# Batch 0 of the one-head layer: its weighted sums by seven block products, and batch 1's norm moved ahead into layer 1's end and batch 0's scores

## The chip, the cores and the metric

The kernel runs on one core of a Trainium2 chip. The metric is the device time of one execution in microseconds (us). The time before is the median of three runs; a profile was taken of one further execution, and every detailed number below comes from that one.

## The reference

Four layers run one after the other on `x`, four batches of 512 channels by 1024 places, all in f32:

```python
x = _L0(x)   # attention with 8 heads of 64, and x added
x = _L1(x)   # linear attention: softplus features, a gate of max + mean, and x added
x = _L2(x)   # layer norm over channels, attention with ONE head of 512, and x added
x = _L3(x)   # group norm, attention with 4 heads of 128, and x added

# _L2, per batch, xf = places x channels
mu = mean(xf, -1);  var = var(xf, -1)
xn = (xf - mu) * rsqrt(var + eps) * norm_w
q, k, v = split(xn @ w_qkv.T + b_qkv)
attn = softmax(q @ k.T * 512 ** -0.5)
out = x + ((attn @ v) @ w_proj.T + b_proj)
```

The change is in layer 2 (`_L2`) and in the end of layer 1 for the last batch.

## The kernel before, in words

**Paths.** `plain_path` computes everything without subtracting row maxima from the scores, and records whether all sums stayed in range; `general_path` follows only where they didn't. With these inputs only `plain_path` runs.

**Block products.** A product of two matrices, each cut into 2 x 2 blocks, is made with seven block products instead of eight, at the price of sums of blocks beforehand and of results afterwards. `seven_products` does this for projections and scores, under the names `p1` to `p7`; within one product the names p5, p6, p7 use sums of blocks on both sides, p3 and p4 on one side. A "join" is the addition of a finished block product to the result (lines L746, L783, L789). Accumulators are PSUM tiles `acc`, four of them; a second pool holds two double tiles, tag `sc`, which the scores, the norm's sums (`lnsums`), and layer 1's steps (`kxt`, `kv`, `upd`) share.

**Order of the work.** TensorE's instructions are issued in exactly the order in which the Python code makes them (`tc.manual_schedule`). The order on the other engines is worked out by the framework's scheduler, which also places the semaphores and frees buffers. Small pieces of another batch's work are put between products through a list, `pieces`: each call of `slot()` inside `seven_products` takes one piece. How many slots there are among the first products (p1 and p2) is set by the parameter `slots`; after each pair of the later ones (p3 to p7) there is always one.

**Around the change.** Layer 1 for batch 3 (`linear_attention`, a list `lin` of pieces) runs as such pieces inside layer 2's start: batch 0's projection of queries and of values. Its last five pieces are `transpose_kx`, `keys_times_values`, an idle one, and two `update`s, which add layer 1's result to `x3`. After them `x3` is written to DRAM (`away`) and batch 1's `x` is read back (`back`)[...].

Layer 2 then goes batch by batch, in `for b in range(B)`: queries by `seven_products` (L716), values by `project_v` (L841), then `one_head`: scores by `seven_products` (L848), exponentials (L1246), and the weighted sums. For batches 1 to 3 the weighted sums are made by a second set of seven products, written out in `one_head` (matmuls at L1325, block sums at L1319, joins at L1335, ScalarE copies at L1339), each of two output columns with four matmuls of 128x512: 7 x 2 x 4 = 56. For batch 0 they are made by a plain loop of eight output blocks with eight matmuls each (L1286): 64. Both are followed or interleaved by two row-sum matmuls (L1265), reciprocals (L687) and the final additions to `x` (L1272, L1274).

**The norm of the next batch.** `layer_norm` for one half of 512 places gives four pieces: `add` (three VectorE additions over the channels, L1588 and L1590), `center` (a TensorE sum, L1596; four VectorE centrings, L1598; ScalarE squares, L1603, summed by VectorE, L1607), `spread` (a TensorE sum, L1612; ScalarE's square root, L1614; VectorE's reciprocal, L1615) and `scale` (four VectorE scalings, L1620). Its results go into tiles `after`, which for batch 1 take the buffers of layer 1's weights. For batch 0 these pieces of batch 1 are put between the eight output blocks of the plain loop, through the list `parts`, since batch 1's `x` is on the chip only then; the last of them makes batch 1's input sums (`sum_inputs`, L695 to L698). For batches 1 and 2 they are put among the projection of values and the scores.

**DMA.** All transfers are issued by SyncE's queue, in its order. Layer 1's transposition sends blocks (`squares`) to DRAM (L1458) and loads them back transposed (L1464).

Of the kernel before, what the change touches and what calls it, by code (L numbers as in the profile page):

```python
# [475 lines left out]
def plain_path(ctx: ExitStack, tc: tile.TileContext, d: dict, out: bass.AP, count):  # L476
# [23 lines left out]
    def acc_tile():  # L500
        return ps_acc.tile([P, TB], F32, tag="acc", name="acc")

    def two_tile(name):
        return ps_sc.tile([P, 2, TB], F32, tag="sc", name=name)
# [4 lines left out]
    def pt_tile(name):  # L509
        return work.tile([P, 2, TB], F32, tag="pt", bufs=4, name=name)  # L510
# [15 lines left out]
    def chunks_tile(tag, name, bufs=1):  # L526
        return work.tile([P, NC, TB], F32, tag=tag, bufs=bufs, name=name)
# [7 lines left out]
    def load_wo(src):  # L535
        t = wpool.tile([P, NC, C], F32, tag="wo", name="wo")
        nc.sync.dma_start(t, src.rearrange("(c p) o -> p c o", p=P))
        return t
# [33 lines left out]
    def away(b):  # L572
        homes[b] = dram.tile([P, NC, S], F32, tag=f"home{b}", bufs=1, name=f"home{b}")
        nc.sync.dma_start(homes[b], xs.pop(b))

    def back(b):
        nc.sync.dma_start(x_tile(b), homes.pop(b))
# [97 lines left out]
    def both(*fs):  # L675
        return lambda: [f() for f in fs]
# [8 lines left out]
    def invert(rd, ps):  # L685

        nc.vector.reciprocal(rd, ps)  # L687
        n, m = next(unit), rd.shape[0]
        for i, t in enumerate((ps, rd)):
            closing[:] = [nc.vector.tensor_reduce(tops[:m, i, n : n + 1], t, AX.X, ALU.max).ins]  # L690
# [532 lines left out]
        while parts:  # L1223
            parts.pop(0)()

    def one_head(b, q, ws, acc, xn, sums, v, scale, bias, room, between, parts):

# [13 lines left out]
        def exp(tb, o):  # L1244
# [12 lines left out]
            lambda: sums,  # L1257
            lambda o: ws,
            keys_first,
            done=exp,  # L1260
        )
        def row_sums():
            rows = two_tile("rowsum")
            for t in range(NTB):
                nc.tensor.matmul(  # L1265
                    rows[:, t, :], lhsT=ones, rhs=acc[:, t, :], start=True, stop=True
                )
            return rows

        def add_block(m, tb, t, source, quotient):  # L1270

            nc.vector.tensor_tensor(t, source, quotient, ALU.mult)  # L1272
            xv = x[:, m, bass.ts(tb, TB)]
            nc.vector.scalar_tensor_tensor(xv, t, bias[:, m : m + 1], xv, ALU.add, ALU.add)  # L1274

        flush()
        between()

        if parts:
            rds = chunks_tile("q0", "rd")  # L1280
            for k, (qb, m) in enumerate(itertools.product(range(NTB), range(NC))):
                if parts:
                    parts.pop(0)()
                out = acc_tile()
                for i, j in enumerate(order):
                    nc.tensor.matmul(  # L1286
                        out, lhsT=v[j // 2][:, j % 2, bass.ts(m, P)], rhs=pts[j][:, qb, :],
                        start=(i == 0), stop=(i == NT - 1),
                    )
                if k == 0:  # L1290
                    rows = row_sums()
                if m == 0:
                    invert(rds[:, qb, :], rows[:, qb, :])
                add_block(m, qb, rds[:, NTB + k % 2, :], out, rds[:, qb, :])
            return

# [279 lines left out]
        ]  # L1578


    def layer_norm(b, tb, tiles):

        x = lambda c: xs[b][:, c, bass.ts(tb, TB)]
        t = {}

        def add():
            s = t["s"] = row_tile("s")
            nc.vector.tensor_tensor(s, x(0), x(1), ALU.add)  # L1588
            for c in range(2, NC):
                nc.vector.tensor_tensor(s, s, x(c), ALU.add)  # L1590

        def center():
            xn = tiles[tb]
            t["ps"] = two_tile("lnsums")
            mean = t["ps"][:, 0, :]
            nc.tensor.matmul(mean, lhsT=ones, rhs=t["s"], start=True, stop=True)  # L1596
            for c in range(NC):
                nc.vector.scalar_tensor_tensor(  # L1598
                    xn[:, c, :], mean, -1.0 / C, x(c), ALU.mult, ALU.add
                )  # L1600
            for c in range(NC):
                sq = row_tile("sq")
                nc.scalar.activation(sq, xn[:, c, :], AF.Square)  # L1603
                if c == 0:
                    t["sq"] = sq
                else:
                    nc.vector.tensor_tensor(t["sq"], t["sq"], sq, ALU.add)  # L1607

        def spread():
            xn = tiles[tb]  # L1610
            var = t["ps"][:, 1, :]
            nc.tensor.matmul(var, lhsT=ones, rhs=t["sq"], start=True, stop=True)  # L1612
            rstd = t["rstd"] = row_tile("rstd")
            nc.scalar.activation(rstd, var, AF.Sqrt, bias=eps, scale=1.0 / C)  # L1614
            nc.vector.reciprocal(rstd, rstd)  # L1615

        def scale():
            xn, rstd = tiles[tb], t["rstd"]
            for c in range(NC):
                nc.vector.scalar_tensor_tensor(  # L1620
                    xn[:, c, :], xn[:, c, :], col("nw2", c), rstd, ALU.mult, ALU.mult
                )

        return [add, center, spread, scale]


# [62 lines left out]
    with tc.manual_schedule(engines={mybir.EngineType.PE}):  # L1689
# [52 lines left out]
        for o in gps:  # L1742
# [10 lines left out]
        loadedv = load_bias(d["bv2"], d["wo2n"], vt[2:], brows[:, 1, :])  # L1753
        flush()
        wo2 = load_wo(d["wo2"])
        lin = linear_attention(B - 1, lambda i: pt_tile("l1"))

        norms[1][0]()
        pieces.extend([
            both(*norms[0][2:]), norms[1][1], *lin[:2], both(*norms[1][2:]), idle, *lin[2:]  # L1760
        ])
        gq = chunks_tile("ot", "gq")
        for o in range(NC):
# [21 lines left out]
        for b in range(B):  # L1785
            q = q_tiles()
            vt = v_tiles()
            after = normed_tiles(b + 1)

            def sums():  # L1790
                if b == 0:
                    made.extend(sum_inputs(spare, normed(xn)))
                return made

            half = NC // 2
            seven_products(
                half,
                lambda i, j, o: gq[:, 2 * j : 2 * j + 2, bass.ts(i * half + o, P)],
                normed(xn),
                lambda i, o: uq[:, i * half + o : i * half + o + 1],  # L1800
                lambda i, tb, o: q[tb][:, i * half + o, :],
                sums,
                slots=2,
            )

            pair = lambda t, i: t[:, 2 * i : 2 * i + 2, :]
            halves = work.tile([P, 2, 2, TB], F32, tag="os", name="qs")
            third = work.tile([P, 2, TB], F32, tag="oi", name="qs")
            places = [halves[:, 0], halves[:, 1], third, pair(q[1], 0)]
            sum_weights(places, lambda i, j: pair(q[i], j))  # L1810
            if b == 0:
                pieces.append(lambda: (away(B - 1), back(1)))
            parts = []
            if b + 1 < B:
                (add0, *n0), (add1, *n1) = [layer_norm(b + 1, tb, after) for tb in range(NTB)]
            if b == 0:

                parts = [
                    both(add0, n0[0]), idle, both(*n0[1:], add1), idle, n1[0], idle,
                    both(*n1[1:]), lambda: sum_inputs(spare, normed(after)),  # L1820
                ]
            elif b + 1 < B:
                pieces.extend([
                    add0, n0[0], idle, n0[1], n0[2], add1, n1[0], idle, n1[1], n1[2],
                ])
            else:
                first = chunks_tile("ot", "gn")
                loaded3 = load_bias(
                    d["bv3"], d["wo3n"], [after[1][:, 2 * i : 2 * i + 2, :] for i in range(2)]
                )  # L1830
                loads3 = []
                pieces.extend([
                    *group_norm(0, 0, first),
                    lambda: loads3.append(weighted_bias("bo3", loaded3)),
                ])
            project_v(vt, hv, normed(xn), made, wpool.tile([P, NC, C], F32, tag="wo", name="ws"))
            one_head(
                b, q, places, work.tile([P, 2, TB], F32, tag="ou", name="acc"), xn, made, vt,
                float(C) ** -0.5, bo2,
                after if b == B - 1 else [w2[:, NC : 2 * NC, :], w2[:, 2 * NC :, :]],  # L1840
                lambda: b + 1 < B or loads3.insert(0, load_wqkv(d["wqkv3"])), parts,
            )
            if 0 < b < B - 1:
                sum_inputs(spare, normed(after))
            away(b)
            back((b + 2) % B)
            if b + 1 < B:
                xn = after
# [103 lines left out]
```

## Time and profile before

| | us |
|---|---|
| median of 3 runs (2434.74 to 2436.24) | 2435.08 |
| the profiled execution | 2434.68 |
| its span in the profile | 2433.0 |
| TensorE busy in the span | 2416.0 |
| VectorE busy | 1497.2 |
| ScalarE busy | 697.6 |
| GpSimd busy | 250.8 |

The span runs from the first to the last instruction in the profile; the rest of the execution's time, 1.68 us, lies around it. Times in the views are in us from the span's start. A line such as `L1286` is a line of the kernel before. Names left of the arrow are what an instruction writes, right of it what it reads; `xN` is how many there are, and a bracket gives the idle time of the engine just before and what ended it. PE is TensorE, DVE VectorE, ACT ScalarE, POOL GpSimd, SPq SyncE's queue. An f32 matmul shows as two records.

### The profile page before, as it was taken

What the parts mean: (1) busy time and instruction counts of PE and PEld (TensorE: products, weight loads), DVE (VectorE), ACT (ScalarE), POOL (GpSimd) and SP (SyncE); (2) the same over time, 40 slices, a digit from 0 to 9 for tenths busy, and PEclk for the clock granted to TensorE, in tenths of its full rate; (3) what the DMA queues carried; (4) which work ended last, traced back from release to release, by engine and by line L of the source; (5) the groups of instructions that cost most, each with busy time, mean ns of one, the idle gap of its engine ahead of it and who ended that gap; (6) DMA issues with size and microseconds to landing.
All of it is one profiled execution on the core that took longest, in us unless ns stands there. A gap on an engine that the chain in (4) does not pass through costs nothing.

```text
span 2433.0 us, 24544 instructions
## 1 busy us (share of the span) xinstructions
PE 2416.0 (99%) x10002; PEld 1203.5 (49%) x10002; DVE 1497.2 (62%) x1786; ACT 697.6 (29%) x860; POOL 250.8 (10%) x240
## 2 busy tenths in 40 slices
PE   9999999999999999999999999999999999999999
PEld 4444544453455344544646446455556446555653
DVE  3678577757875789556595775754453554445344
ACT  1454154406431643121211302013321330322132
POOL 4001100110020002102103021021020001002000
PEclk9999999999999999999999999999999999999999
DMA  5001120211022121111001020110110011001001
GB/s 186 9 11 42 46 79 17 55 61 44 19 77 87 58 58 53 44 52 69 1 0 69 5 87 0 52 70 18 35 70 0 18 35 52 1 35 35 1 22 45
DMA packets 41900, 104.35 MB, mean 43 GB/s; under 512 B 3419, under 2 KB 19291, under 8 KB 38838
## 3 DMA queue, kind: packets, MB, share of 16 engines
q1 hardware_dynamic: 41782, 102.73, 12.5%
q8 instruction: 80, 1.31, 0.2%
q14 instruction: 38, 0.31, 0.0%
HBM read 68.98 MB, written 33.74 MB: 42 GB/s over the span
## 4 chain that ended last, share of the span: by engine, by line
PE 98%; DVE 1%; ACT 1%; issue 0%; DMA 0%; SPq 0%; DVEq 0%
PE acc L716 19%; PE acc L841 12%; PE acc L976 9%; PE acc L991 9%; PE sc L945 9%; PE sc L940 9%; PE acc L848 8%; PE acc L1093 7%; PE acc L1325 6%; PE acc L1286 2%; PE acc L1027 1%; PE acc L650 1%; PE upd L1553 1%; PE acc L1493 1%; PE kv L650 1%; PE feat L650 1%
## 5 line engine op out<-in xcount | busy, mean ns | idle before, releaser
L950 ACT ACTIVATE pt<-sc 128x1024 f32<-128x1024 f32 x384 | 379.2, 1022 | 541.2 <-PE sc L945 304.0
L959 DVE TENSOR_TENSOR sum<-sum,pt 128x1024 f32<-128x1024 f32 x256 | 314.4, 1228 | 159.3 <-ACT pt L950 147.2
L976 PE MATMUL acc<-pt,v 64*64 64x512 f32 x2048 | 248.4, 591 | 0.0
L940 PE MATMUL sc<-q,k 64*64 64x512 f32 x2048 | 245.5, 591 | 1.1 <-ACT pt L950 1.1
L991 PE MATMUL acc<-pt,v 128*128 128x512 f32 x512 | 240.8, 594 | 0.0
L945 PE MATMUL sc<-q,k 128*128 128x512 f32 x512 | 239.8, 593 | 0.0
L716 PE MATMUL acc<-t,ws 128*128 128x512 f32 x384 | 173.9, 593 | 0.0
L704 POOL TENSOR_TENSOR ws<-wqkv 128x256 f32<-128x256 f32 (+1 forms) x40 | 39.2, 981 | 1296.7 <-PE acc L1027 516.1
L956 DVE TENSOR_TENSOR sum<-pt 128x1024 f32<-128x1024 f32 x64 | 78.0, 1219 | 137.4 <-ACT pt L950 137.4
L991 PEld LDWEIGHTS acc<-pt,v 128*128 128x128 f32 x512 | 96.6, 190 | 125.3 <-issue 121.6
L945 PEld LDWEIGHTS sc<-q,k 128*128 128x128 f32 x512 | 96.8, 190 | 116.2 <-issue 93.1
L976 PEld LDWEIGHTS acc<-pt,v 64*64 64x64 f32 x2048 | 77.5, 133 | 143.9 <-issue 141.1
L940 PEld LDWEIGHTS sc<-q,k 64*64 64x64 f32 x2048 | 76.9, 133 | 141.8 <-issue 132.9
L716 PEld LDWEIGHTS acc<-t,ws 128*128 128x128 f32 x384 | 72.7, 190 | 88.0 <-issue 87.3
L755 ACT COPY v<-acc 128x512 f32<-128x512 f32 x24 | 14.0, 585 | 305.2 <-PE acc L841 305.2
L687 DVE RECIPROCAL rd<-acc 128x512 f32<-128x512 f32 (+1 forms) x24 | 80.5, 3353 | 29.1 <-PE acc L1027 29.1
L841 PE MATMUL acc<-ws,t 128*128 128x256 f32 x384 | 86.8, 379 | 0.0
L848 PE MATMUL acc<-qs,w 128*128 128x512 f32 x192 | 86.3, 592 | 0.0
L848 PE MATMUL acc<-q,ln 128*128 128x512 f32 x192 | 85.8, 593 | 0.0
L1093 PE MATMUL acc<-ot,wo 128*128 128x256 f32 x336 | 80.6, 383 | 2.7 <-ACT ou L1112 2.7
L746 DVE TENSOR_TENSOR v<-acc,v 128x512 f32<-128x512 f32 x72 | 49.6, 690 | 53.7 <-PE acc L841 53.6
L755 ACT COPY q<-acc 128x512 f32<-128x512 f32 x40 | 23.4, 585 | 195.8 <-PE acc L716 195.8
(323 smaller groups left out, 3420.1 us busy)
## 6 DMA issues: line engine op xcount, KB each, us to landing
home<-x SPq DMA_DIRECT2D x8, 2048.0 KB
x<-home SPq DMA_DIRECT2D x8, 2048.0 KB
squares<-squares SPq DMA_DIRECT2D x32, 256.0 KB
out<-x SPq DMA_DIRECT2D x32, 256.0 KB
rds<-quotients SPq DMA_DIRECT2D x30, 256.0 KB
rds<-quotients SPq DMA_DIRECT2D x7, 1024.0 KB
x<-in_x SPq DMA_DIRECT2D x3, 2048.0 KB
v<-squares SPq DMA_DIRECT2D x12, 512.0 KB
```

Of the source, the lines that this page charges most:

```text
L687: nc.vector.reciprocal(rd, ps)
L716: nc.tensor.matmul(ps, lhsT=w[:, m, :], rhs=x[:, m, :], start=start, stop=stop, skip_group_check=True)
L841: nc.tensor.matmul(ps[:, bass.ts(r, C // 2)], lhsT=x[:, m, bass.ts(2 * o + r, P)], rhs=w[:, m, :], start=(start and r == 0), stop=stop, sk ...
L848: nc.tensor.matmul(ps, lhsT=x[:, m, bass.ts(o, P)], rhs=w[:, m, :], start=start, stop=stop, skip_group_check=True,)
L940: nc.tensor.matmul(ps[half(h), s, :], lhsT=key(g, i)[half(s), half(h)], rhs=q[qb][half(s), g, :], start=True, stop=True,)
L945: nc.tensor.matmul(ps[:, s, :], lhsT=key(g, 2 * i + s), rhs=q[qb][:, g, :], start=True, stop=True)
L950: exps.append(nc.scalar.activation(pt, ps, AF.Exp, scale=scale).ins)
L959: adds.append(nc.vector.tensor_tensor(acc, acc, pt, ALU.add).ins)
L976: nc.tensor.matmul(outs[qb, g][r][half(s), :], lhsT=v[i // 2][half(r), i % 2, g * P + s * hd : g * P + (s + 1) * hd], rhs=pt[half(r), s, : ...
L991: nc.tensor.matmul(outs[qb, g][0], lhsT=v[j // 2][:, j % 2, bass.ts(g, P)], rhs=pt[:, s, :], start=(j == 0), stop=(j == NT - 1),)
L1093: nc.tensor.matmul(ps[i][:, bass.ts(o, n)], lhsT=w[:, m, bass.ts(o, P)], rhs=t[:, m, :], start=(start and m + o == 0), stop=(stop and m == ...
L1325: nc.tensor.matmul(ps[i, o], lhsT=w[m][:, bass.ts(o, P)], rhs=t[m], start=(start and m == 0), stop=(stop and m == 3), skip_group_check=True,)
```

## The change

1. The plain loop over eight output blocks in `one_head` is gone, and with it the parameter `parts`. All four batches take the seven products.
2. Batch 1's norm reads copies of batch 1's `x` instead of the `x` tile. `copy_next` reads one half from DRAM into a buffer, 1 MB each: the first into the buffer of layer 0's shared quotients (tag `rds`), the second into that of layer 1's transposed blocks (tag `many`).
3. The norm's pieces stand among layer 1's last five pieces, in batch 0's projection of values, and among the first products of batch 0's scores. The write of `x3` and the read of batch 1's `x` come after the second half's centring.
4. The scores get four more slots (`slots=NC`), in every batch. Batches 1 and 2 keep their list of norm pieces, so its last ones come at those slots.
5. The norm's two sums take a PSUM tile each instead of sharing one.
6. Batch 1's input sums are made after `one_head`, as for the later batches.

```diff
-    def one_head(b, q, ws, acc, xn, sums, v, scale, bias, room, between, parts):
+    def one_head(b, q, ws, acc, xn, sums, v, scale, bias, room, between):
...
             keys_first,
+            slots=NC,
             done=exp,
         )
...
-        if parts:
-            rds = chunks_tile("q0", "rd")
-            for k, (qb, m) in enumerate(itertools.product(range(NTB), range(NC))):
-                if parts:
-                    parts.pop(0)()
-                out = acc_tile()
-                for i, j in enumerate(order):
-                    nc.tensor.matmul(
-                        out, lhsT=v[j // 2][:, j % 2, bass.ts(m, P)], rhs=pts[j][:, qb, :],
-                        start=(i == 0), stop=(i == NT - 1),
-                    )
-                if k == 0:
-                    rows = row_sums()
-                if m == 0:
-                    invert(rds[:, qb, :], rows[:, qb, :])
-                add_block(m, qb, rds[:, NTB + k % 2, :], out, rds[:, qb, :])
-            return
...
-    def layer_norm(b, tb, tiles):
-        x = lambda c: xs[b][:, c, bass.ts(tb, TB)]
+    def layer_norm(b, tb, tiles, copies=None):
+        x = lambda c: copies[tb][:, c, :] if copies else xs[b][:, c, bass.ts(tb, TB)]
...
-            t["ps"] = two_tile("lnsums")
-            mean = t["ps"][:, 0, :]
+            mean = two_tile("lnsums")[:, 0, :]
...
-            var = t["ps"][:, 1, :]
+            var = two_tile("lnsums")[:, 0, :]
...
+        copies = []
+
+        def copy_next(t):
+            nc.sync.dma_start(t, homes[1][:, :, bass.ts(len(copies), TB)])
+            copies.append(t)
+
+        copy_next(work.tile([P, NC, TB], F32, tag="rds", name="x1"))
         lin = linear_attention(B - 1, lambda i: pt_tile("l1"))
...
-            both(*norms[0][2:]), norms[1][1], *lin[:2], both(*norms[1][2:]), idle, *lin[2:]
+            both(*norms[0][2:]), norms[1][1], *lin[:2], both(*norms[1][2:]), idle, *lin[2:-5]
...
+            if b == 0:
+                (add0, *n0), (add1, *n1) = [
+                    layer_norm(1, tb, after, copies) for tb in range(NTB)
+                ]
+                transpose_kx, keys_times_values, _, *updates = lin[-5:]
+                pieces.extend([
+                    both(transpose_kx, add0),
+                    both(keys_times_values, lambda: copy_next(many_tile("x1"))), n0[0], *updates,
+                    n0[1], both(n0[2], add1), both(n1[0], lambda: (away(B - 1), back(1))), idle,
+                    *n1[1:],
+                ])
...
-            if b == 0:
-                pieces.append(lambda: (away(B - 1), back(1)))
-            parts = []
-            if b + 1 < B:
+            if 0 < b < B - 1:
                 (add0, *n0), (add1, *n1) = [layer_norm(b + 1, tb, after) for tb in range(NTB)]
-            if b == 0:
-                parts = [
-                    both(add0, n0[0]), idle, both(*n0[1:], add1), idle, n1[0], idle,
-                    both(*n1[1:]), lambda: sum_inputs(spare, normed(after)),
-                ]
-            elif b + 1 < B:
                 pieces.extend([
                     add0, n0[0], idle, n0[1], n0[2], add1, n1[0], idle, n1[1], n1[2],
                 ])
-            else:
+            elif b > 0:
...
-            if 0 < b < B - 1:
+            if b < B - 1:
                 sum_inputs(spare, normed(after))
```

More of the change, by code (lines that the diff above doesn't have):

```diff
@@ L1840, in plain_path @@
                 after if b == B - 1 else [w2[:, NC : 2 * NC, :], w2[:, 2 * NC :, :]],
-                lambda: b + 1 < B or loads3.insert(0, load_wqkv(d["wqkv3"])), parts,
+                lambda: b + 1 < B or loads3.insert(0, load_wqkv(d["wqkv3"])),
             )
-            if 0 < b < B - 1:
+            if b < B - 1:
                 sum_inputs(spare, normed(after))
```

## The prediction

> **What bounds the kernel now.** I read the page's busy times and chain first, then the order in time of TensorE and VectorE around layer 2's first batch, then SyncE's queue. From the page:
>
> ```profile
> PE 2416.0 (99%) x10002; PEld 1203.5 (49%) x10002; DVE 1497.2 (62%) x1786; ACT 697.6 (29%) x860; POOL 250.8 (10%) x240
> ...
> PE 98%; DVE 1%; ACT 1%; issue 0%; DMA 0%; SPq 0%; DVEq 0%
> ```
>
> TensorE is the bound almost everywhere: work taken from it counts in full, work given to others counts only where TensorE comes to wait. Busy times by stage: columns are length, then busy us (count) of TensorE, weight loads, VectorE, ScalarE, GpSimd, then clock and DMA.
>
> ```profile
> 1007.00:1048.00 41.00, 41.00 (x139) 23.82 (x138) 16.51 (x23) 5.27 (x9) 0.00 (x0) 1.00 0.26 103
> 1048.00:1078.00 30.00, 30.00 (x72) 13.26 (x71) 18.59 (x26) 8.68 (x8) 0.00 (x0) 1.00 0.00 1
> 1078.00:1138.00 60.00, 60.00 (x142) 26.52 (x141) 48.12 (x55) 8.72 (x12) 2.77 (x3) 1.00 0.00 0
> 1238.00:1288.00 50.00, 50.00 (x117) 21.97 (x117) 41.68 (x57) 2.92 (x4) 4.95 (x5) 1.00 0.00 0
> ```
>
> Rows one and two are the end of layer 1 and batch 0's scores, row three its weighted sums by eight products, row four batch 1's by seven. TensorE is full in all four: seven products already run here without a hole. TensorE in order of time (start, duration, line, records):
>
> ```profile
> 1077.48 1.02 PE L1596 MATMUL lnsums<-s,ones 128*128 128x512 f32 x2
> 1078.34 5.31 PE L1286 MATMUL acc<-pt,v 128*128 128x512 f32 x12
> ...
> 1137.56 7.03 PE L716 MATMUL acc<-ln,gq 128*128 128x512 f32 x16
> ...
> 1188.36 1.12 PE L1596 MATMUL lnsums<-s,ones 128*128 128x512 f32 x2 [0.71 <-DVE s L1590]
> ...
> 1238.25 2.74 PE L1325 MATMUL acc<-pt,v 128*128 128x512 f32 x6
> ...
> 1253.70 3.60 PE L1325 MATMUL acc<-w 128*128 128x512 f32 x8
> ...
> 1288.17 7.03 PE L716 MATMUL acc<-ln,gq 128*128 128x512 f32 x16
> ```
>
> An f32 matmul is two records. Starts, not durations, give its price: batch 1's 56 products and two row sums fill 1238.25 to 1288.17, 49.92 / 58 = 0.86 us each. Batch 0's 64 products, two row sums and three norm sums (69) fill 1078.34 to 1137.56: 59.22 / 69 = 0.858. The bracket at 1188.36 is the one hole in layer 2's batches.
>
> VectorE, in order of time:
>
> ```profile
> 1178.05 3.35 DVE L1615 RECIPROCAL rstd<-rstd 128x512 f32<-128x512 f32 x1 [0.29 <-ACT rstd L1614]
> ...
> 1186.90 1.41 DVE L1590 TENSOR_TENSOR s<-s,x 128x512 f32<-128x512 f32 x2
> ...
> 1235.13 0.68 DVE L746 TENSOR_TENSOR pts<-acc,pts 128x512 f32<-128x512 f32 x1
> ...
> 1249.10 1.42 DVE L1319 TENSOR_TENSOR v<-v,w 128x256 f32<-128x256 f32 x4
> ```
>
> In batch 1 the sums that the norm's mean needs (L1590) stand behind a reciprocal: hence the hole. The seven products' own sums end at 1249.10 + 1.42 = 1250.5, 3.2 us before the first product that needs them (1253.70). SyncE's queue:
>
> ```profile
> 957.62 2.87 SPq L1458 DMA_DIRECT2D squares<-squares  x4
> 960.58 23.07 SPq L1464 DMA_DIRECT2D l<-squares  x4
> ```
>
> [...] (a record shows 592 ns, two start within 858), so I price by starts. [...] four loads at L1464 take SyncE 23.07 us, so a new copy's wait would hold up what follows.
>
> **The change, part by part.**
> (1) 64 products become 56. Row and norm sums keep their number; the issue order has exactly 8 matmuls of 128x512 fewer. 8 x 0.858 = -6.87 us, all on the path.
> (2) The seven products need 16 sums of 128x256 (0.42 us), 16 of 128x512 and 10 joins (0.685): 6.7 + 17.8 = 24.5 us of VectorE, and two ScalarE copies (0.58). Cover: the norm leaves this stretch. A half of it is 3 adds, 4 centrings, 3 square sums (10 x 0.685), a reciprocal (3.35) and 4 scalings (0.68 to 0.9): 13 to 14 us, two halves 27. So VectorE's 18.59 + 48.12 changes by about -2.5.
> (3) Those 27 us move to about 1011 to 1059. There the first row has VectorE busy 16.51 of 41 and GpSimd idle. Cover exists, if each piece is in time.
> (4) Two copies of 1 MB from DRAM, on SyncE's queue. The first goes out once the last shared quotient is read (L1060, 897.5 to 898.7), ahead of loads that left at 902.6; free. The second stands ahead of the four L1464 loads and waits for the block writes issued at 957.62 to 960.5. DMA activity there dies by about 966, first load included. 2 MB take 6.3 us (layer 1's write issued 1031.07, its read 1037.39), so 1 MB is estimated at 3 to 4 us: the first load lands near 971; its products start at 991.55. The second load waits for softplus (near 980) anyway. Price 0, from both sides: no wait is there to be removed, and 20 us of lateness are free.
> (5) Batch 3's write back and batch 1's read move behind the norm. With copies nobody needs that x before batch 1's additions (from 1264). Free.
> (6) Four more slots in the scores. In batches 1 and 2 the second variance comes 8 matmuls after its mean (6.87 us) instead of 24. In batch 2 VectorE's squares were summed at 1344.4, mean finished at 1338.95: 5.5 needed, 1.4 spare. Free.
> (7) In the changed VectorE order batch 1's mean sums stand ahead of the reciprocal, as they already do in batch 2, where TensorE has no hole. The 0.71 us go: -0.71.
> (8) Batch 1's input sums (L695 to L698) no longer come inside batch 0's last products but among its final additions; batches 1 and 2 do this already without a hole. Free.
>
> **The new waits in batch 0,** from the issue orders with the durations above. TensorE, each start the one before plus 0.858 (f32, 512 columns) or 0.43 (256) per matmul: first mean at 1018.3, first updates 1022.6, first variance 1033.3, second mean 1041.0, second variance 1048.8, weighted sums from 1080.5. VectorE fits the first adds into its 2.9 us idle before the key-value step at 1015. The first centrings free a PSUM pair at 1022.4; the second update needs it at 1023.5. First squares at 1024.8: 8 us early. Second adds at 1034.4: 6.6 early. Second squares at 1047.4: 1.4 early. Behind the second reciprocal (1050.5 to 1053.9) stand the joins of p6 and p5; p3 of column 0 needs p5's by 1056.5: 1053.8, p6's join 0.6, p5's 0.6, ready at 1055.0. At the end p3 of the last column, at 1078.8, needs the join of p5, which ends on TensorE at 1077.1. VectorE, free at 1076.8, has two new sums (0.6 each) in front of it, so the join runs 1078.0 to 1078.6: 0.2 spare, against 0.7 in batch 1 (join from 1235.13, p3 from 1236.53). I take 0.1 us of waiting for all of them; the bounds are 0, as nothing waits here now so there is no gain to be had, and about 5 (each of five places a whole late addition or two). The seven products' sums end near 1088; needed at 1096.
>
> Sum: -6.87 - 0.71 + 0.1 = -7.5. Span 2433.0 to 2425.5; that execution's 2434.68 (1.68 around its span) to 2427.2; the median 2435.08, 0.4 above it, to 2427.6.
>
> **Rivals.** (A) Small waits in batch 0's scores. For: VectorE's order is tight (0.2, 1.1, 1.4). Against: each is short and batch 1 has the same pattern. 2 to 5 us lost: 2429.6 to 2432.6, say 2431. (B) VectorE becomes the bound of the weighted sums: the scores' joins slip and the sums with them. For: 42 of 50 us busy in batch 1. Against: 8 us spare. If p6 waits 7 us, the saving is eaten: about 2435. (C) Slower: the second copy blocks SyncE. If its buffer comes free late, the four block loads leave late and layer 1's key products wait at 991.55. It decides where the second load leaves after about 985 + 12.5 us (saving plus 0.2%), 34 later than the block writes land; at 45 later TensorE waits some 23 us: 2450. Against: the buffer's readers are just those block writes. (D) The products stay eight: excluded, the instruction count shows 8 fewer.
>
> **Chances.** Forecast 0.72 (own range 2426 to 2429.5), A 0.15, B 0.05, C 0.05, 0.03 for a larger gain. What a measurement can tell from no change is 0.2%, 4.9 us: below 2430.2 is faster, above 2440 slower. Faster: 0.72 + 0.03 + a third of A = 0.80; slower: C and a tail, 0.06; same 0.14. The range 2425.5 to 2432 leaves out B, C and A's upper end.
>
> **What would show it.** TensorE full from 1007 to the end of batch 0's weighted sums, which take about 49.8 us instead of 59.2; the hole at batch 1's second mean gone; the L1464 line's loads still ending near 983; norm sums of batch 1 between 1018 and 1050. Wrong if brackets naming VectorE appear at lnsums or acc products there, if p3 of the last column waits, or if key products wait for DMA.

## The result and the profile after

| | before | after |
|---|---|---|
| median, us (9 runs of each, side by side) | 2435.66 (2434.69 to 2436.85) | 2428.38 (2427.94 to 2429.06) |
| the profiled execution, us | 2434.68 | 2428.28 |
| its span, us | 2433.0 | 2426.6 |
| TensorE busy, us (records) | 2416.0 (10002) | 2409.3 (9986) |
| VectorE busy, us (instructions) | 1497.2 (1786) | 1520.1 (1828) |

The ratio is 0.997, with a 95% interval of 0.9962 to 0.9979: 7.3 us faster. The prediction was 2427.6 us, 7.5 us faster.

First the page of the kernel after: its busy times, and the shares of the chain that ended last. In every view below, line numbers are those of the kernel that the view is of.

```profile
PE 2409.3 (99%) x9986; PEld 1200.5 (49%) x9986; DVE 1520.1 (63%) x1828; ACT 700.3 (29%) x863; POOL 251.6 (10%) x240
...
PE 98%; DVE 1%; ACT 0%; DMA 0%; issue 0%; SPq 0%; DVEq 0%
```

Sixteen records fewer are eight matmuls fewer. VectorE has 22.9 us more to do and the chain hardly notices: it is TensorE's as before.

Busy times by stage of the kernel after, in the columns of the prediction's table: end of layer 1, batch 0's scores, batch 0's weighted sums, and batch 1's weighted sums.

```profile
1007.00:1048.00 41.00, 41.00 (x140) 24.15 (x140) 33.10 (x45) 11.90 (x19) 0.00 (x0) 1.00 0.26 103
1048.00:1080.00 32.00, 32.00 (x76) 14.11 (x75) 29.30 (x43) 8.31 (x8) 0.00 (x0) 1.00 0.00 1
1080.00:1131.00 51.00, 51.00 (x120) 22.48 (x119) 41.77 (x56) 3.29 (x4) 4.56 (x4) 1.00 0.00 0
1229.00:1281.00 52.00, 52.00 (x122) 22.91 (x121) 42.38 (x56) 3.29 (x4) 4.90 (x5) 1.00 0.00 0
```

TensorE is full in all four. In the first row VectorE goes from 16.51 to 33.10 us: that is the norm. The third row now looks like the fourth.

TensorE in order of time, the kernel after:

```profile
962.24 3.60 PE L716 MATMUL acc<-ln,gq 128*128 128x512 f32 x8
...
1019.03 1.02 PE L1581 MATMUL lnsums<-s,ones 128*128 128x512 f32 x2
...
1049.91 1.02 PE L1597 MATMUL lnsums<-sq,ones 128*128 128x512 f32 x2
...
1079.95 1.88 PE L848 MATMUL acc<-q,ln 128*128 128x512 f32 x4
1081.66 2.74 PE L1308 MATMUL acc<-pt,v 128*128 128x512 f32 x6
...
1131.59 1.88 PE L716 MATMUL acc<-ln,gq 128*128 128x512 f32 x4
...
1181.51 1.02 PE L1581 MATMUL lnsums<-s,ones 128*128 128x512 f32 x2
...
2416.54 3.96 PE L1162 MATMUL out<-ot,wo 128*128 128x512 f32 x8
```

No line between 1000 and 1600 us carries a bracket: none of the four sums of batch 1's norm makes TensorE wait. Nor does the sum at 1181.51, which has lost its 0.71 us; it is the second mean taken during batch 1, for batch 2's norm, and is called "batch 1's second mean" below. On VectorE its sums now stand ahead of the reciprocal:

```profile
1171.82 1.42 DVE L1576 TENSOR_TENSOR s<-s,x 128x512 f32<-128x512 f32 x2
...
1173.75 3.34 DVE L1600 RECIPROCAL rstd<-rstd 128x512 f32<-128x512 f32 x1
```

The weighted sums run from 1081.66 to 1131.59, 49.93 us; before they took 59.22, with three of the norm's sums (2.6 us) among them, which now stand earlier.

The first and the last of these lines give a ruler that leaves out the start of the kernel, where the profiled executions differ: TensorE's wait for the first load of weights from DRAM was 4.34 us in the kernel before and 4.84 in the kernel after. From batch 0's first query products to the last output products it is 2416.54 - 962.24 = 1454.30 us. In the kernel before it is:

```profile
961.48 3.60 PE L716 MATMUL acc<-ln,gq 128*128 128x512 f32 x8
...
2423.51 3.96 PE L1162 MATMUL out<-ot,wo 128*128 128x512 f32 x8
```

that is 1462.03, so the change took 7.73 us from the path. The spans differ by only 6.4, because in the profiled execution of the kernel after everything ahead of 962 happened to be 0.76 us later, already so at 890 us, and what follows the last output products took 0.57 us longer. Below, "the path" is this stretch in each kernel's profiled execution. Three kernels that should equal the changed one gave 1454.31 to 1454.32, one profile each, so it shows tenths, where the runs of one kernel spread over one to three microseconds.

### The profile page after: what moved, and what is told of

It is laid out like the page before. It is cut to its first block, busy times and chain, and to the rows that moved or that the text cites. A ratio compares the mean times of both kernels' runs of the same rounds, so it can differ in the third digit from the quotient of the medians.

```text
span 2426.6 us, 24549 instructions
## 1 busy us (share of the span) xinstructions
PE 2409.3 (99%) x9986; PEld 1200.5 (49%) x9986; DVE 1520.1 (63%) x1828; ACT 700.3 (29%) x863; POOL 251.6 (10%) x240
## 4 chain that ended last, share of the span: by engine, by line
PE 98%; DVE 1%; ACT 0%; DMA 0%; issue 0%; SPq 0%; DVEq 0%
PE acc L716 19%; PE acc L841 12%; PE acc L976 9%; PE acc L991 9%; PE sc L945 9%; PE sc L940 9%; PE acc L1308 8%; PE acc L848 8%; PE acc L1093 7%; PE acc L1027 1%; PE acc L650 1%; PE upd L1536 1%; PE acc L1476 1%; PE kv L650 1%; PE feat L650 1%; PE feat L1400 0%
## 5 line engine op out<-in xcount | busy, mean ns | idle before, releaser
L841 PE MATMUL acc<-ws,t 128*128 128x256 f32 x384 | 86.8, 379 | 0.0
```

The costliest lines, as they stand in the source:

```text
L841: nc.tensor.matmul(ps[:, bass.ts(r, C // 2)], lhsT=x[:, m, bass.ts(2 * o + r, P)], rhs=w[:, m, :], start=(start and r == 0), stop=stop, sk ...
```

## The experiments

Path times are differences from the kernel after, 1454.30 us.

| kernel | median, us | path, us | new holes of TensorE, us |
|---|---|---|---|
| before | 2435.66 | +7.73 | 0.71 |
| after | 2428.38 | 0 | none |
| eight products, norm early | 2435.18 | +6.81 | none |
| seven products, norm late | 2447.51 | +19.92 | 8.64, 6.50, 0.71 |
| extra slots in batch 0 alone | 2428.38 | +0.02 | none |
| no extra slots | 2436.60 | +7.74 | 4.93 |
| copy repeated 3 times | 2428.22 | +0.02 | none |
| copy repeated 7 times | 2440.97 | +12.39 | 10.98 |
| 8 more block sums | 2428.18 | +0.01 | none |
| 24 more block sums | 2442.72 | +13.46 | 11.78 |
| GpSimd's sums later, from after | 2426.61 | -1.55 | one of 1.16 less |
| GpSimd's sums later, from before | 2434.44 | +6.24 | one of 1.16 less than before |

**What the eight products are worth.** The norm stays early, the copies and slots stay; batch 0's weighted sums go back to the plain loop.

```diff
+        if b == 0:
+            rds = chunks_tile("q0", "rd")
+            for k, (qb, m) in enumerate(itertools.product(range(NTB), range(NC))):
+                out = acc_tile()
+                for i, j in enumerate(order):
+                    nc.tensor.matmul(out, lhsT=v[j // 2][:, j % 2, bass.ts(m, P)],
+                        rhs=pts[j][:, qb, :], start=(i == 0), stop=(i == NT - 1))
...
+            return
```

> The changed kernel, but batch 0 of the 1-head layer makes its weighted sums by the plain eight-product loop again; the next batch's norm stays early, among the scores, with both copies of x1. Theory (the gain is the eight products saved, 8 x 0.858 us, plus the 0.71 us hole): this gives the 6.87 us back, 2428.4 + 6.9 = 2435.3 us, and the trace shows 64 weighted-sum products in batch 0, the three norm sums still before them, and no new hole. Rival (the gain comes from taking the norm's waits out of the weighted sums, the products were only its occasion): the time stays under 2432 us.

Measured 2435.18 us, the path 6.81 us longer: 8 x 0.858 = 6.87. The rival, that the gain came from clearing the norm out of the weighted sums, falls: that move alone, with eight products, brings 7.73 - 6.81 = 0.92 us. The hole at batch 1's second mean stays away, so it doesn't depend on the seven products; the line carries no bracket:

```profile
1187.49 1.02 PE L1597 MATMUL lnsums<-s,ones 128*128 128x512 f32 x2
```

**What the norm's move is worth.** The seven products stay, but batch 1's norm goes back among the weighted-sum products and reads the `x` tile; copies and extra slots go. Batch 1's input sums stay behind `one_head`, where the change has put them.

```diff
-            slots=NC,
...
+        part()
         p1(0)
         p1(1)
...
+            if (f, o) in ((p6, 0), (p6, 1), (p4, 0), (p3, 0), (p4, 1)):
+                part()
             f(o)
...
-                    layer_norm(1, tb, after, copies) for tb in range(NTB)
+                parts = [
+                    both(add0, n0[0]), idle, both(*n0[1:], add1), idle, n1[0], idle, both(*n1[1:]),
+                ]
```

> The changed kernel's seven products in batch 0, but the next batch's norm left where the kernel before had it, between the weighted-sum products, without the copies of x1. Theory (the move of the norm is what pays for the added VectorE work): from 1048 to 1131 us VectorE then has about 18.6 us of joins, 48.1 us of eviction and sums already there, 24.5 us of new block sums and up to 27 us of norm, more than the 83 us that there are, so TensorE waits in batch 0's weighted sums or at the products that read the norm after them: 2432 to 2445 us, with VectorE at or near full in that stretch. Rival (the cover was never needed, there is slack in the stretch before and after): 2428 to 2430 us.

Measured 2447.51 us, slower than the kernel before by 12, a little beyond the expected range. TensorE's holes in order of time:

```profile
1117.58 2.04 PE L1588 MATMUL lnsums<-s,ones 128*128 128x512 f32 x2 [8.64 <-DVE s L1583]
1119.42 4.46 PE L1307 MATMUL acc<-ts,v 128*128 128x512 f32 x8
...
1155.27 8.80 PE L716 MATMUL acc<-w,ws 128*128 128x512 f32 x16 [6.50 <-DVE w L696]
...
1200.98 1.12 PE L1588 MATMUL lnsums<-s,ones 128*128 128x512 f32 x2 [0.71 <-DVE s L1583]
```

and VectorE ahead of the first of them:

```profile
1107.84 3.35 DVE L1607 RECIPROCAL rstd<-rstd 128x512 f32<-128x512 f32 x1
1111.10 0.63 DVE L1317 TENSOR_TENSOR ln<-ln,acc 128x512 f32<-128x512 f32 x1
1111.64 2.73 DVE L1612 SCALAR_TENSOR_TENSOR ln<-ln,cols,rstd 128x512 f32<-128x512 f32 x4
1114.29 0.69 DVE L1581 TENSOR_TENSOR s<-x 128x512 f32<-128x512 f32 x1
```

The second mean's sums stand behind the first half's reciprocal and scalings, and VectorE is busy from 1094.39 us, when the row sums arrive, up to there, but for 0.24 us. It isn't the amount of block sums by itself that makes this hole: they were done at 1093.1, and VectorE then stood idle for 1.21 us. From the row sums on it has their two reciprocals with what follows them, and then the norm: 23 us of work, while the second mean was due 14.5 us after the row sums, at 1108.9.

The second hole stands before batch 1's query products, which need its input sums (L695 to L698). These come late, as the norm's second half ends only at 1144.5. But part of that lateness has another cause:

```profile
1144.42 2.89 DVE L1272 TENSOR_TENSOR ln<-ln 128x512 f32<-128x512 f32 x2
1147.23 3.42 DVE L1274 SCALAR_TENSOR_TENSOR x<-ln,bo,x 128x512 f32<-128x512 f32 x2
1150.57 2.28 DVE L695 TENSOR_TENSOR w<-ln 128x1024 f32<-128x1024 f32 x1
```

In the kernel before one of these took 0.69, 0.75 and 1.22 us. Here they run beside sums of weights on GpSimd (busy 6.74 us from 1140 to 1148 and 3.69 from 1148 to 1155.3) and take 4.5 us longer in all. The collision is one that this order brought about; how long the second hole would be without it was not measured.

The three holes are 15.85 us; nearly all of the other 4 come from products that ran slowly after these holes. The matmuls of the mean after 8.64 us take 2.04 us instead of 1.02 and the eight records behind them 4.46 instead of 3.60; the sixteen after 6.50 us take 8.80 instead of 7.03.

**Which part of the change removes the 0.71 us, and what the extra slots do.** Two kernels: the extra slots in batch 0 only, and in no batch.

```diff
-            slots=NC,
+            slots=NC if b == 0 else 0,
```

> The changed kernel with the reserved slots of the score products (slots=NC) for batch 0 alone. Theory (the reservation costs nothing anywhere and gains nothing in the other batches): 2428.4 us, within 0.4. Rival (the 0.71 us hole at batch 1's second mean went because of the reservation in the later batches, not by the norm's two separate PSUM tiles): the hole is back at about 1181 us in the trace and the time is 2429.1 us.

```diff
-            slots=NC,
+            slots=0,
```

> The changed kernel without the four extra slots among the scores' first products, in any batch: batch 1's second mean and variance then come 20 to 30 products later in batch 0's scores, and their squares, reciprocal and scalings fall among the last joins and the first sums of blocks of the seven products. Theory (the extra slots aren't free to leave out: they keep the norm's second half away from those sums): TensorE waits in batch 0's last scores or first weighted sums, 2430 to 2435 us, and batch 1 has no hole at its second mean, as that went with the norm's early place and not with the slots. Rival (the slots do nothing): 2428.4 us within 0.5; or, if the hole of 0.71 us at batch 1's second mean returns, the slots were what removed it.

With slots in batch 0 alone nothing changes: 2428.38 us, the path within 0.02. In batches 1 and 2 they are neutral. Without any, the whole gain is gone: 2436.60 us. That is above the expected 2430 to 2435, so the size was underestimated. TensorE in the kernel without slots:

```profile
1068.06 2.07 PE L1597 MATMUL lnsums<-sq,ones 128*128 128x512 f32 x2 [4.93 <-DVE sq L1592]
1069.93 8.66 PE L848 MATMUL acc<-qs,w 128*128 128x512 f32 x16
```

and its VectorE in the same place:

```profile
1063.85 0.68 DVE L1592 TENSOR_TENSOR sq<-sq 128x512 f32<-128x512 f32 x1
1064.45 1.22 DVE L1248 TENSOR_TENSOR acc<-pt 128x1024 f32<-128x1024 f32 x1
1065.59 0.69 DVE L1592 TENSOR_TENSOR sq<-sq 128x512 f32<-128x512 f32 x1
1066.19 1.22 DVE L1248 TENSOR_TENSOR acc<-acc,pt 128x1024 f32<-128x1024 f32 x1
```

The second half's variance now comes in the middle of the scores, where VectorE weaves its square sums with the row sums of exponentials, and TensorE, whose order is fixed, waits 4.93 us at that one matmul. After it the variance's sum takes 2.07 instead of 1.02 us and sixteen records 8.66 instead of 7.03, another 2.7 us. The hole at batch 1's second mean does not come back in either kernel, nor with eight products; with the norm late (two PSUM tiles for its sums, as in the change) it is there. So neither the slots nor the seven products are needed to remove it, and two PSUM tiles alone don't: it goes with the early place of batch 1's norm and its copies, in whose company the scheduler puts the sums for batch 1's second mean ahead of the reciprocal. Why its order turns there was not traced further.

**How much lateness the copies have.** The first copy is repeated into the same buffer, between layer 1's last block writes and its four loads, each repeat waiting for the one before; the loads are kept behind the last.

```diff
+        def again(last):
+            for _ in range(3):                 # or 7
+                with tc.issue_after(last):
+                    last = nc.sync.dma_start(copies[0], homes[1][:, :, :TB]).ins
+            return last
...
-        lin = linear_attention(B - 1, lambda i: pt_tile("l1"))
+        lin = linear_attention(B - 1, lambda i: pt_tile("l1"), again)
```

> The changed kernel with the first copy of batch 1's x repeated three times (same data, same buffer) on SyncE's queue between layer 1's last block writes and its four transposed loads, each repeat waiting for the one before. At an estimated 4.5 to 6 us each the first load leaves 14 to 18 us later than the 965 us it left at, before the 20 us of lateness are used up, and the second load waits for the softplus until 981 us anyway. Theory (a copy ahead of the loads costs nothing up to about 20 us): 2428.4 us, within 0.5. Rival (the copies were only just free): 2430 us or more, with TensorE waiting at layer 1's key products.

> The same with seven repeats: 32 to 42 us, so the loads leave at 997 to 1007 us and the first lands 3 to 4 us later, at 1001 to 1011, while its key products are due at 992.3. Theory (past 20 us of lateness each microsecond counts): TensorE waits 8 to 18 us for the load at the key products (and some more, as the products after a long hole ran slower elsewhere), 2437 to 2448 us, which is what the rival C of the prediction would have cost. Rival (the key products aren't on the path, or the transfers overlap): under 2431 us.

With three the time is 2428.22 us:

```profile
960.99 1.20 SPq L1759 DMA_DIRECT2D x<-home  x1
...
974.85 9.26 SPq L1454 DMA_DIRECT2D l<-squares  x4
```

The loads left only 9.6 us later (974.85 instead of 965.26), not 14 to 18, since the first repeat went out right behind the block writes, ahead of the change's own second copy. So this kernel shows 9.6 us to be free, and not yet 20. With seven it is 2440.97 us, slower than the kernel before (ratio 1.0022, 1.0013 to 1.0030). SyncE's queue with seven:

```profile
964.43 0.52 SPq L1752 DMA_DIRECT2D x<-home  x1
968.91 27.41 SPq L1759 DMA_DIRECT2D x<-home  x6
996.36 2.79 SPq L1454 DMA_DIRECT2D l<-squares  x4
```

and TensorE:

```profile
1003.16 3.26 PE L1483 MATMUL acc<-l,kf 128*64 128x512 f32 x8 [10.98 <-DMA l<-squares]
```

A 1 MB copy that waited for the one before held the queue 27.41 / 6 = 4.57 us here; the 4.5 to 6 of the expectations was the author's estimate. The loads left at 996.4, and TensorE waited for them at layer 1's key products: 10.98 us of hole, 12.39 on the path. As the loads left 31.1 us later than in the kernel after, an estimate from these two figures is that 20 us of lateness were free.

**How much room VectorE has under the seven products.** Batch 0's four sums `t1` are made more than once: 8 or 24 more additions of 128x512.

```diff
-        each(t1, inputs(0, 1), inputs(0, 0), ALU.subtract)
+        for _ in range(3 if b == 0 else 1):    # or 7
+            each(t1, inputs(0, 1), inputs(0, 0), ALU.subtract)
```

> The changed kernel with the four sums t1 of batch 0's weighted sums made three times instead of once: 8 VectorE additions of 128x512 more, 4.8 us. In the changed kernel VectorE had its sums ready at 1092.7 us and then nothing to do for 4.65 us, and the first product that needs them starts at 1097.1. Theory (VectorE has 4 to 8 us of room there): 2428.4 us, within 0.5. Rival (VectorE is already at the bound, rival B of the prediction): 2431 us or more, with holes of TensorE from 1056 to 1110 us.

> The same sums made seven times: 24 additions, 14.4 us more. Theory (8 to 9 us of room between the sums that the sixth product needs, done at 1088.4, and its start at 1097.1): TensorE loses 5 to 12 us in batch 0's weighted sums, 2433 to 2441 us. Rival (more than 14 us of room): 2429 us or less.

The 8 additions, 4.8 us at 0.60 each from start to start (six of the repeated sums take 3.61 us, from 1088.12 to 1091.73, in the kernel with 24 more), cost nothing: 2428.18 us. In the kernel after VectorE has this idle time before the row sums arrive:

```profile
1091.92 0.75 DVE L1302 TENSOR_TENSOR v<-v,w 128x256 f32<-128x256 f32 x2
1097.32 3.36 DVE L687 RECIPROCAL ln<-rowsum 128x512 f32<-128x512 f32 x1 [4.65 <-PE rowsum L1266]
```

14.4 us more cost 13.46 on the path, beyond the 5 to 12 expected. VectorE with 24 more, in order of time:

```profile
1098.36 0.69 DVE L1302 TENSOR_TENSOR w<-pts,ts 128x512 f32<-128x512 f32 x1
1098.96 3.35 DVE L687 RECIPROCAL ln<-rowsum 128x512 f32<-128x512 f32 x1
...
1103.96 3.35 DVE L687 RECIPROCAL ln<-rowsum 128x512 f32<-128x512 f32 x1
...
1112.21 1.89 DVE L1302 TENSOR_TENSOR pt<-pt 128x512 f32<-128x512 f32 x3
```

The sums for the first product that needs any were still in time: they end at 1099.05, and no hole stands before it. But by then the row sums were ready, and their two reciprocals with what follows them went ahead of the second group of sums: 1098.96 to 1110.87, 12 us in one piece, and TensorE shows one hole in front of the products that read that group:

```profile
1112.95 4.37 PE L1308 MATMUL acc<-pt,w 128*128 128x512 f32 x6 [11.78 <-DVE pt L1302]
```

The room is about 4.65 us of idle time. The loss beyond it is more than the work beyond it (14.4 - 4.65 = 9.75 us), since a whole group went ahead: a step rather than a slope. Where between 8 and 24 additions it lies was not measured.

**The 1.16 us hole at 981 us.** Both kernels have it, at the same product and of the same length. In the kernel after, four scalings on VectorE run ahead of it beside GpSimd's sums of the value weights:

```profile
963.12 6.27 DVE L1605 SCALAR_TENSOR_TENSOR ln<-ln,cols,rstd 128x512 f32<-128x512 f32 x4
...
963.76 1.72 POOL L704 TENSOR_TENSOR ws<-w 128x512 f32<-128x512 f32 x1
...
981.20 1.98 PE L716 MATMUL acc<-w,gq 128*128 128x512 f32 x4 [1.16 <-DVE q L789]
```

On VectorE the input sums, the softplus and the join that the product waits for stand behind the scalings.

The edit lets GpSimd begin after the softplus, by a tiny operation that reads its result:

```diff
-        ws = sum_weights([halves[:, i] for i in range(NC)], weights)
+        with nullcontext() if mark is None else tc.issue_after(
+            nc.gpsimd.tensor_tensor(mark, feat[:, :1], feat[:, :1], ALU.add).ins
+        ):
+            ws = sum_weights([halves[:, i] for i in range(NC)], weights)
```

> The changed kernel with one thing added: in batch 0 GpSimd's sums of the value weights wait, by a tiny operation that reads the softplus result, until about 984 us, so that they no longer run beside VectorE's four scalings of the norm at 962 us (6.3 us there where the same four take 2.7 us elsewhere). Theory (contention between GpSimd and VectorE makes the softplus late and so makes the 1.16 us hole at 981 us): the four scalings take about 2.7 us, the hole goes, 2427.3 us. Rival (the hole has another cause, or the contention only moves to the additions after the softplus): 2428.4 us or more, with the hole where it was or a new one before 1010 us.

> The kernel before, with only the late start of GpSimd's sums of the value weights in batch 0 that took the changed kernel from 2428.4 to 2426.6 us. Theory (the 1.16 us hole at 981 us and the slow scalings ahead of it have nothing to do with the change): the same 1.8 us, 2433.8 us, no hole there, and the four scalings at 2.7 us. Rival (the gain needs the changed kernel's order): 2435.4 us or more.

From the kernel after it gives 2426.61 us (2426.07 to 2426.97), the fastest of all, ratio 0.9963 to the kernel before (0.9949 to 0.9976). VectorE there:

```profile
962.79 2.74 DVE L1608 SCALAR_TENSOR_TENSOR ln<-ln,cols,rstd 128x512 f32<-128x512 f32 x4
```

The four scalings take 2.74 us, and TensorE has no hole from 960 to 1300 us. GpSimd's sums take 1.27 us each at their new place, where three of the four took 1.60 to 1.72 in the kernel after. From the kernel before, the median falls by 1.0 us only, short of what was expected (2433.8; the kernel before had 2435.4 beside it), but its path shortens by 7.73 - 6.24 = 1.49 us, as the other's by 1.55; the medians, each spread over 1 to 3 us, don't tell these apart. The gain is independent of the change.

## Why the prediction was right, point by point

(1) Eight products, -6.87 us: the path shows 6.81 when they are put back. This is the gain.

(2) 24.5 us more on VectorE, covered because the norm leaves: VectorE is 22.9 us busier on the whole and TensorE has no hole. That the norm must leave is shown: with it left in the stretch the change would have cost 12 us. But the cover was not as the step worked it out. It had VectorE's work in the two stretches, 18.59 + 48.12 us, change by -2.5; it is 29.30 + 41.77, 4.4 more in 7 us less time, mainly since the second half's reciprocal and scalings still lie in batch 0's scores. By the trace, the first wait that the late norm brought came from its place behind the row sums more than from the total: the argument from busy time reached the right answer without naming that wait.

(3) Norm moved to 1011 to 1059: its four sums stand at 1019.03 to 1049.91, 0.7 to 1.2 us after the predicted times, most of it the 0.76 us of the later start.

(4) Two copies at price 0: right. SyncE's loads end at 984.40 instead of 983.65, again the later start. A copy that waited for its predecessor held the queue 4.57 us, more than the 3 to 4 estimated for one copy. Rival C said that the change would end 0.2% slower than the kernel before if the second load left after about 997.5 us. That was nearly met: with the four loads leaving from 996.4 to 999.2 it was 0.22% slower.

(5) and (8) had no cost that the trace shows.

(6) "Four more slots: free" was true for the batches that the step looked at, and missed what they are for. In batch 0 the deadlines of the section on new waits hold only thanks to those slots; without them 7.74 us are lost, all of the gain. The prediction put no price on leaving them out.

(7) The hole at batch 1's second mean: -0.71, right. With the 6.81 of (1) it makes 7.52 of the path's 7.73; 0.1 more is the matmul that ran slower after its hole, and the last 0.1 is not accounted for. It was not the one hole in layer 2's batches, as the prediction says: the 1.16 us at 981 stand before batch 0's query products, in both kernels.

The new waits in batch 0, 0.1 us: none is seen. The steps reckoned with stand in the traces: 0.43 us per matmul of 256 columns (L841 in the kernel before, 16 from 1178.85 to 1185.76), 0.60 us from one VectorE sum of 128x512 to the next (L1302 in the kernel after, 1085.83, 1086.43, 1087.03). The second variance has its squares summed at 1048.5 and starts at 1049.91, 1.4 spare as predicted. Two other margins were mis-sized without harm. The last join ends at 1079.22 and its p3 starts at 1079.95: 0.7 spare where 0.2 was forecast, because TensorE reached it 0.4 us later and VectorE 0.1 earlier than worked out, once the later start is taken off. The seven products' sums are all done at 1092.67; near 1088 only those of the first product that needs any were. The 8 us of room claimed against rival B are rather 4.65, with a step of 12 somewhere behind it.

So the sum was right, and its two terms that save were right for the reasons given. Its weak place was that several parts of the change (norm, slots) were priced only as costs, at nothing, and not as conditions of the gain.

## What to carry to other kernels

When an engine off the bound takes on work, price the parts that make room for it as well as those that save: here the saving was 6.8 us, but leaving the norm where it was cost 19.9 and leaving out four slots 7.7. Look for what the added work will stand behind, not only for the total: VectorE had idle time in the kernel with the late norm too, but hardly any between the row sums and the mean. Measure the path between two instructions of the bounding engine, not the span: it repeated within 0.02 us over four kernels here while their starts differed by 0.6. And cover can end in a step: in the run with 24 more sums, work that came late fell behind the next long group on VectorE, and TensorE's hole, 11.78 us, was about that group's length, 12 us.

## What the runs showed of the hardware

In these runs each hole of 4.93 us or more cost more than its length. After 4.93 us without work TensorE had a granted clock of 0.50 for 5 us. Windows of the kernel without slots, before and after its hole ends (the clock is the third column from the end):

```profile
1062.00:1068.00 6.00, 1.13 (x3) 0.19 (x1) 6.00 (x10) 4.44 (x5) 0.00 (x0) 0.86 0.00 0
1068.00:1073.00 5.00, 4.94 (x6) 2.18 (x7) 5.00 (x12) 1.97 (x2) 0.00 (x0) 0.50 0.01 3
```

TensorE had gone idle at 1063.13. If the clock was either full or 0.50, the mean of 0.86 over the first window's 6 us makes 1.7 us at 0.50; so by this estimate it fell 3.2 us into the hole. The same estimate gives 3.2 us for the hole of 6.50 (0.77 from 1148 to 1155.3), 4.6 for that of 11.78 (0.74 from 1100 to 1112) and 5.4 for that of 8.64 (0.81 from 1109 to 1117.6), so the runs give no one figure for it.

The extra over the durations of the same products elsewhere was 2.7 us after 4.93, 1.8 after 6.50, 1.9 after 8.64, 1.3 after 10.98 and 1.6 after 11.78; it was 0.1 after 0.71 or 1.16. From the mean clocks of the windows behind three of them (0.64 over 4.70 us after 6.50, 0.60 over 4.40 after 8.64, 0.80 from 1112 to 1122 after 11.78), the half clock is estimated to have lasted 3.4, 3.5 and 3.0 us into the work, and the extra is about half of that. The extra does not grow with the hole: it is largest after the shortest of the five. No run has a hole between 1.16 and 4.93 us, so how long a hole must be before it loses this is not shown more closely.

VectorE's four scalings took 6.27 us beside GpSimd's sums and 2.74 without them, and three of GpSimd's sums 1.60 to 1.72 each beside the scalings and 1.27 without. One after the other, the four scalings and these three sums would take 2.74 + 3 x 1.27 = 6.55 us, and together they took 6.27, from 963.12 to 969.39: side by side they were hardly faster than in turn. What makes them slow these durations don't show.
